# Loading each 128-row block of x in two half-width transfers instead of one

## The chip, the cores and the metric

The kernel runs on one core of one Trainium2 chip. The metric is the device time of one execution in microseconds (us), as a median over runs. A core has five engines with a queue of instructions each: PE (matrix multiplication, whose weight loads are listed as PEld), DVE, ACT, POOL and SP. SP computes nothing here; its queue issues nearly all plain transfers between DRAM and the on-chip memory. POOL issues the indexed transfers (scatter and gather). All transfers are carried out by 16 DMA engines.

## The reference, cut to what matters

`x` is 32 batches of 512 rows (channels) by 1024 columns (nodes), in float32, that is 2.1 MB a batch; `adj` is 512 by 512.

```python
q = einsum('c,bcn->bn', wq, x);  k = einsum('c,bcn->bn', wk, x)
scores = q[:, None, :] + k[:, :, None]
att = softmax(where(scores > 0, scores, 0.01 * scores), axis=-1)
agg = einsum('bcn,bmn->bcm', x, att)
x = layernorm(x + relu(einsum('oc,bcm->bom', adj, agg) + bm[None, :, None]))
x = layernorm(x + einsum('bnf,nm->bmf', x, adj * adj) + bias)
```

## The kernel before, in words

The batches are handled one after the other, with the steps of about four batches interleaved. The softmax over 1024 nodes is not done as a matrix: because a score is the sum of one number per row and one per column, the kernel sorts the nodes by `q`, makes running sums of the sorted rows from both ends, and looks up for each row the place where the score changes sign.

For one batch the steps are as follows. `load` (`ld` in the schedule, line 87) brings x into a tile of 128 partitions by 4 blocks by 1024 columns, one transfer for each block of 128 rows, 512 KB each, issued from SP. `parts` (`pa`, line 247) multiplies x with `wq` and `wk` on PE: block 0 first, then blocks 1, 2 and 3, and within a block four column groups of 256, which PE runs side by side in four quarters of its array. ACT copies the result (`pc`, line 255), SP writes it out and reads it back to all partitions (`qw` and `ro`, lines 275 and 283), and DVE and ACT compute ranks and counts from it (`rk`, line 308, and `ct`, line 323). PE computes `z`, adj times x, transposed (`z`, line 346, and the steps beginning with `z` at line 390, which are a seven-product scheme for half of the columns). POOL scatters the rows of z to their ranks in DRAM (`sc`, line 451). SP reads the sorted rows back (`sl`, line 470), DVE forms the running sums (lines 491 and 501), SP writes them as a table (`tw`, line 553), POOL gathers two entries per node (`g`, line 563), DVE and ACT mix them (`mix`, lines 585 and 590), and PE transposes the mixture (`t`, line 609). DVE adds it to x in place (line 617), ACT normalises x (line 635), and the second layer follows: its sums of quarters on DVE (`T1` to `T4`, lines 646 to 660), its seven-product scheme on PE (lines 667 and 702), its residual, its normalisation, and the store (`st`, line 777).

The order on every engine is written out by hand in three strings of words, `head` (start and batches 0 to 13), `loop` (batches 14 to 18) and `tail`. A word such as `ld.1` calls `load` for the batch one later than the current one. The change doesn't touch these strings, so the words stay in their order.

Three things set when a load can run. The pool `xp` has four tiles, so the load of a batch reuses the tile of the batch four earlier, and its first transfer waits on SP until the last readers of that tile are done, among them `T4` on DVE (line 660) and the last products of the second layer on PE (line 667). The words `ld.1` and `pa.1` stand about 8 us apart in time, so PE asks for the new x soon after. And all plain transfers take turns on eight completion counters: a transfer's issue waits until the transfer eight earlier has landed. Ahead of the loop, where four loads follow one another, these counters hold back the issue.

A part of the loop that shows the load and its neighbours:

```python
    mw.-2.1 t4.-3 ms.-2.4 12.-3.0 ms.-2.6 up.-3.1 ms.-2.7 Y.-3.0 d.-1.4 ld.1 s1.-3.1 mx.-2.6
    zc.0.1 ra.-3.1 Y.-3.1 zc.0.0 lr.-3.0 rb.-3.1 ms.-2.5 up.-3.0 r1.-3.1 sc.0.1 21.-3.0 lr.-3.1
    s1.-3.0 sc.0.0 mx.-2.5 d.-1.3 21.-3.1 ll.-3.0 ra.-3.0 mx.-2.7 n.-3.1 rb.-3.0 d.-1.2 cu.-1
    r1.-3.0 mx.-2.4 ll.-3.1 st.-3.1 d.-1.1 pa.1 uc.-1 ls.-3.1 ls.-3.0 d.-1.0 s1.-3.3 tu.-1.0
```

Of the kernel before, what the change touches and what calls it, by code (L numbers as in the profile page):

```python
# [42 lines left out]
P = 128  # L43
# [6 lines left out]
def adj_resnorm_kernel(  # L50
# [10 lines left out]
    nc = tc.nc  # L61
# [3 lines left out]
    H = 512  # L65
# [18 lines left out]
    def load(b):  # L84
        t = xp.tile([P, CT, N], F32, tag="x", name=f"x_{b}")
        for c in range(CT):
            nc.sync.dma_start(out=t[:, c, :], in_=x[b, c * P : (c + 1) * P, :])
        xts[b] = t


# [16 lines left out]
    for h in range(2):  # L107
        nc.scalar.dma_start(
            out=room[3 - 3 * h : 6 - 3 * h, 0, :],
            in_=bias[h * H : (h + 1) * H].partition_broadcast(3),  # L110
# [665 lines left out]
    def store(b, m):  # L776
# [5 lines left out]
    ops = {  # L782
        "ldw": adj_load, "wt": adj_turn, "wc": adj_copy_odd, "wd": adj_copy_even, "R": adj_sums,
        "ld": load, "pa": parts, "pc": parts_copy, "co": cols, "cc": cols_copy, "ro": row,
        "tb": top, "tp": top_end, "qw": row_out, "rk": rank, "re": rank_end, "ct": count, "ce": count_end,
        "we": weights_exp, "oq": own_q, "z": product, "zc": product_copy, "sc": scatter,
# [497 lines left out]
```

## Time and profile before

| what | value |
|---|---|
| median of 3 runs | 1942.7 us (1941.02 to 1945.48) |
| the profiled execution's own time | 1937.53 us |
| its span | 1935.6 us |
| PE busy | 1887.7 us, 98% of the span |
| DVE / ACT / POOL busy | 1702.7 / 1483.2 / 894.1 us |
| moved by the DMA engines | 558.05 MB, 288 GB/s over the span |
| loads of x | 128 transfers of 512 KB |

The span runs from the first to the last instruction of the profiled execution; 1.9 us of its own time lie around it. An engine that is busy for nearly the whole span can still be held up for short times that matter. The chain of work that ended last tells where: it is followed back from the last instruction to whatever released each step. A queue named q1 carries the plain transfers of SP, q10 those of ACT, and q0 the scatters and gathers of POOL. The records of the DMA engines are packets; a packet of a load of x is one row of one block, 4096 bytes.

### The profile page before, as it was taken

What the parts mean: (1) busy time and instruction counts of PE and PEld (TensorE: products, weight loads), DVE (VectorE), ACT (ScalarE), POOL (GpSimd) and SP (SyncE); (2) the same over time, 40 slices, a digit from 0 to 9 for tenths busy, and PEclk for the clock granted to TensorE, in tenths of its full rate; (3) what the DMA queues carried; (4) which work ended last, traced back from release to release, by engine and by line L of the source; (5) the groups of instructions that cost most, each with busy time, mean ns of one, the idle gap of its engine ahead of it and who ended that gap; (6) DMA issues with size and microseconds to landing.
All of it is one profiled execution on the core that took longest, in us unless ns stands there. A gap on an engine that the chain in (4) does not pass through costs nothing.

```text
span 1935.6 us, 23404 instructions
## 1 busy us (share of the span) xinstructions
PE 1887.7 (98%) x7073; PEld 1072.8 (55%) x7073; DVE 1702.7 (88%) x2746; ACT 1483.2 (77%) x2663; POOL 894.1 (46%) x1074
## 2 busy tenths in 40 slices
PE   7989999999999999999999999999999999999897
PEld 3654556555555555556555556555565555564343
DVE  6898899998899889989988989988999989898983
ACT  3566778888778777778887778877778787877786
POOL 5263535335535345444456444455453455445531
PEclk9999999999999999999999999999999999999999
DMA  6577788777788687877787877777888677887862
GB/s 251 199 296 279 273 330 329 268 293 284 294 332 317 252 309 270 327 297 306 288 305 277 317 305 304 288 297 284 310 310 314 259 294 294 311 316 279 336 244 94
DMA packets 147446, 558.05 MB, mean 288 GB/s; under 512 B 19653, under 2 KB 19793, under 8 KB 139129
## 3 DMA queue, kind: packets, MB, share of 16 engines
q1 hardware_dynamic: 89784, 353.87, 48.3%
q0 software_dynamic: 57344, 202.15, 27.6%
q8 instruction: 56, 0.92, 0.2%
q14 instruction: 70, 0.57, 0.1%
q10 hardware_dynamic: 192, 0.55, 0.1%
HBM read 287.08 MB, written 269.42 MB: 288 GB/s over the span
## 4 chain that ended last, share of the span: by engine, by line
PE 83%; DMA 7%; DVE 5%; ACT 2%; issue 2%; POOL 1%; SPq 0%; DVEq 0%; POOLq 0%; ACTq 0%
PE z_ps L346 20%; PE sum_ps L667 19%; PE pair_ps L667 10%; PE z_sum_ps L390 10%; PE z_pair_ps L390 7%; PE agg_ps L609 5%; PE pair_ps L702 5%; PE qk_ps L247 3%; DMA x<-in_x_dram 2%; DMA table<-tab 2%; DMA tab<-sorted_z 2%; PE carry_ps_False L509 1%; DVE tab L538 1%; PE carry_ps_True L509 1%; DVE junk_v L308 1%
## 5 line engine op out<-in xcount | busy, mean ns | idle before, releaser
L563 POOL DMA_INDIRECT got<-table,of x256 | 302.9, 1183 | 565.5 <-DMA table<-tab 226.2
L346 PE MATMUL z_ps<-adj_t,x 128*128 128x512 f32 x1088 | 486.8, 594 | 1.7 <-ACT adj_t L179 1.0
L451 POOL DMA_INDIRECT sorted_z<-zt,to x256 | 314.9, 1230 | 177.8 <-issue 75.1
L308 DVE SCALAR_TENSOR_TENSOR junk_v<-qb,qkc,tie 128x1024 uint8<-128x1024 f32 x256 | 328.7, 1284 | 12.3 <-DMA x<-in_x_dram 6.7
L346 PEld LDWEIGHTS z_ps<-adj_t,x 128*128 128x128 f32 x1088 | 202.3, 190 | 225.6 <-issue 210.7
L323 ACT ACTIVATE junk_s<-qb,qkc 128x1024 uint8<-128x1024 f32 x256 | 293.4, 1146 | 22.1 <-DMA qb<-q_row 14.1
L667 PE MATMUL sum_ps<-zt,S 128*128 128x512 f32 x512 | 236.1, 593 | 2.3 <-DVE zt L651 1.2
L585 ACT ACTIVATE got<-got,w 128x512 f32<-128x512 f32 x256 | 172.6, 718 | 42.5 <-DVE w L580 42.1
L590 DVE SCALAR_TENSOR_TENSOR got<-got,w 128x512 f32<-128x512 f32 x256 | 185.8, 747 | 11.0 <-ACT got L585 10.6
L491 DVE SCALAR_TENSOR_TENSOR tab<-tab,ac 128x514 f32<-128x514 f32 x192 | 144.7, 753 | 45.4 <-ACT tab L486 29.5
L617 DVE SCALAR_TENSOR_TENSOR x<-agg_ps,small,x 128x1024 f32<-128x1024 f32 x128 | 163.2, 1281 | 23.1 <-PE agg_ps L609 22.8
L600 ACT ACTIVATE junk<-g,tv 128x1024 uint8<-128x1024 f32 x128 | 146.9, 1148 | 34.9 <-DVE g L722 28.6
L501 DVE SCALAR_TENSOR_TENSOR tab<-tab,ac 128x513 f32<-128x513 f32 x224 | 167.8, 749 | 2.3 <-ACT tab L499 1.5
L667 PEld LDWEIGHTS sum_ps<-zt,S 128*128 128x128 f32 x512 | 96.5, 190 | 120.7 <-issue 106.6
L753 POOL TENSOR_SCALAR tv<-tv 128x1 f32<-128x1 f32 x124 | 51.5, 415 | 239.7 <-ACT junk L600 233.6
L774 ACT ACTIVATE g<-g,nb,tv 128x1024 f32<-128x1024 f32 x124 | 151.1, 1237 | 8.2 <-POOL nb L764 8.1
L600 ACT ACTIVATE junk<-x,tv 128x1024 uint8<-128x1024 f32 x128 | 146.9, 1148 | 12.2 <-DVE x L617 9.9
L538 DVE TENSOR_TENSOR tab<-tab,carry 128x2052 f32<-128x2052 f32 x64 | 146.3, 2292 | 4.1 <-ACT carry L516 4.1
L635 ACT ACTIVATE x<-x,tv 128x1024 f32<-128x1024 f32 x128 | 139.3, 1141 | 0.5
L609 PEld LDWEIGHTS agg_ps<-ident,got 128*128 128x128 f32 x1024 | 116.4, 141 | 36.2 <-issue 24.5
L609 PE MATMUL agg_ps<-ident,got 128*128 128x128 f32 x1024 | 129.3, 273 | 2.7 <-DVE g L722 2.0
L667 PE MATMUL sum_ps<-x,adj 128*128 128x512 f32 x256 | 123.4, 605 | 7.2 <-ACT x L635 7.2
(144 smaller groups left out, 3280.9 us busy)
## 6 DMA issues: line engine op xcount, KB each, us to landing
table<-tab SPq DMA_DIRECT2D x64, 2056.0 KB
tab<-sorted_z SPq DMA_DIRECT2D x64, 1028.0 KB
x<-in_x_dram SPq DMA_DIRECT2D x128, 512.0 KB
out_dram<-g SPq DMA_DIRECT2D x128, 512.0 KB
qb<-q_row SPq DMA_DIRECT2D x31, 512.0 KB
sorted_z<-zt,to POOLq DMA_INDIRECT x256, 5.1
got<-table,of POOLq DMA_INDIRECT x256, 7.9
adj_in<-in_adj_dram SPq DMA_DIRECT2D x1, 1024.0 KB
```

Of the source, the lines that this page charges most:

```text
L308: nc.vector.scalar_tensor_tensor(s.junk, s.qb, s.q[:, j : j + 1], tie[:, at : at + N], ALU.subtract, ALU.is_gt, accum_out=s.rank[:, j : j ...
L323: nc.scalar.activation(junk, s.qb, AF.Sign, bias=s.k[:, j : j + 1], accum_out=s.sign[:, j : j + 1])
L346: nc.tensor.matmul(s.z[j], xt[:, c, j * P : (j + 1) * P], adj_t[:, c, :], start=(c == 0), stop=(c == CT - 1),)
L390: nc.tensor.matmul(ps, a[:, i, k * P : (k + 1) * P], v[:, i, :], start=start and i == 0 and (k == 0 or bank == 1), stop=(i == 1), skip_gro ...
L451: nc.gpsimd.indirect_dma_start(out=sorted_z[b % 2][:, :], out_offset=bass.IndirectOffsetOnAxis(ap=s.to[:, j : j + 1], axis=0), in_=zt[:, j ...
L501: nc.vector.scalar_tensor_tensor(v, v, c, s.zs[:, j + 1, 0:D], ALU.mult, ALU.add)
L563: nc.gpsimd.indirect_dma_start(out=s.got[:, j, :], out_offset=None, in_=table[b % 2][:, :], in_offset=bass.IndirectOffsetOnAxis(ap=s.of[:, ...
L585: nc.scalar.activation(down, down, AF.Copy, scale=s.w[:, 1, j : j + 1])
L590: nc.vector.scalar_tensor_tensor(up, up, s.w[:, 0, j : j + 1], down, ALU.mult, ALU.add)
L600: nc.scalar.activation(junk, t, AF.Square, bias=v[0][:, i : i + 1], scale=-float(N), accum_out=v[1][:, i : i + 1],)
L609: nc.tensor.transpose(s.agg[o][:, j * P : (j + 1) * P], s.got[:, j, o * P : (o + 1) * P], ident)
L667: nc.tensor.matmul(ps, a[:, k, g * P : (g + 1) * P], v[:, k, :], start=False, stop=(k == 1), skip_group_check=first is None,)
```

## The change

Each block of 128 rows is loaded by two transfers, one for columns 0 to 511 and one for columns 512 to 1023, in place of one transfer of whole rows. A batch takes eight transfers of 256 KB in place of four of 512 KB. The bytes, the destination and the order of all other instructions stay as they are.

```diff
         for c in range(CT):
-            nc.sync.dma_start(out=t[:, c, :], in_=x[b, c * P : (c + 1) * P, :])
+            for h in range(2):
+                at = slice(h * H, (h + 1) * H)
+                nc.sync.dma_start(out=t[:, c, at], in_=x[b, c * P : (c + 1) * P, at])
         xts[b] = t
```

`H` is 512 and `CT` is 4.

## The prediction

> **What bounds the kernel now.** I read the page first: the busy times, then the chain that ended last.
>
> ```profile
> PE 1887.7 (98%) x7073; PEld 1072.8 (55%) x7073; DVE 1702.7 (88%) x2746; ACT 1483.2 (77%) x2663; POOL 894.1 (46%) x1074
> ...
> PE 83%; DMA 7%; DVE 5%; ACT 2%; issue 2%; POOL 1%; SPq 0%; DVEq 0%; POOLq 0%; ACTq 0%
> ```
>
> PE is nearly always at work and holds 83% of the chain. The table of busy times by stretches shows where its 48 idle us lie: 10 us before 40 us, 9 us between 100 and 180 us, 27 us after 1760 us. In the middle there is nothing left (columns: stretch, its length, then the busy us of PE, PEld, DVE, ACT and POOL with instruction counts, PE's clock, the DMA engines' share, GB/s):
>
> ```profile
> 700.00:1300.00 600.00, 599.66 (x2309) 345.75 (x2308) 542.03 (x870) 478.81 (x856) 295.56 (x339) 1.00 0.79 298
> ```
>
> So a change to the loads counts only where PE would wait for x. The view of line 87 gives what waits today (us, times), and the chain around one such place shows the mechanism (start, length, what):
>
> ```profile
> L87 SPq DMA_DIRECT2D x<-in_x_dram x128: 328/430/1140, 0.8 to 1747.9; - x128
> ...
>   PEld qk_ps L247: 2.1, 4
>   PE qk_ps L247: 0.3, 1
> ```
>
> ```profile
> 925.82 3.45 PE pair_ps L667 x8
> ...
> 929.32 0.35 SPq L87
> ...
> 930.66 7.77 DMA x<-in_x_dram
> 938.44 0.04 issue
> 938.48 0.64 PE qk_ps L247 x8
> 939.12 3.63 PE z_ps L346 x8
> ```
>
> The fourth transfer is issued at 930.66 and lands at 938.44, and PE, in the middle of `parts`, begins its block 3 at that moment. The load is just in time. How nearly so elsewhere can be worked out from the landing events in the trace. In the three loads that PE waits for, the time from PE's first matmul of line 247 to the landing is longer than 1.25 us by just the delay that PE shows, so block 3 is needed 1.25 us after that matmul. Over the 28 loads from batch 4 on, the landing comes 0.68 us before this (median): six have under 0.5 us to spare, nine between 0.5 and 0.8 us, ten more, and three are late, by 0.27, 0.49 and 0.30 us (batches 17, 23, 31). This margin of 0.7 us is what the change spends or spares.
>
> The time line of an ordinary batch shows what shares the DMA engines with the load:
>
> ```profile
> 1104.29 1.77 SPq L87 DMA_DIRECT2D x<-in_x_dram  x4
> 1107.07 1.08 POOL L451 DMA_INDIRECT sorted_z<-zt,to  x1 [0.42 <-ACT got L585]
> 1108.45 1.49 POOL L451 DMA_INDIRECT sorted_z<-zt,to  x1 [0.21 <-issue]
> 1111.25 0.34 SPq L777 DMA_DIRECT2D out_dram<-g  x1
> 1111.89 1.93 PE L247 MATMUL qk_ps<-x,wqk 128*32 128x256 f32 x32
> ```
>
> Two scatters are issued 2.8 and 4.2 us after the load's start. In the DMA records their packets begin about 7.0 us after the load's start; the load's packets end at 7.1 us on the middle DMA engine and at 8.0 us on the last.
>
> **The change part by part.**
>
> *Issue on SP.* Four more issues per load. The first of a row takes 0.35 us, the others 0.43, with 0.04 between (above: four in 1.77 us). Eight take 0.39 + 7 x 0.47 = 3.7 us, 1.9 us more. Behind them on SP stands the store of line 777, issued 7.0 us after the load's start and waiting for ACT, so 3.3 us remain of that cover; without it the store would come 1.9 us later, and nobody waits for it. Does the later issue delay the landing? A first 512 KB transfer lands 3.5 us after its issue and the next ones 1.28 us apart, so some 2.2 us are fixed. The eighth, issued at 3.2 us, would alone land at about 3.2 + 2.2 + 0.65 = 6.1 us; the stream is done at 7.4 us at the earliest. The issue doesn't decide. Cost: nothing.
>
> *Smaller packets.* Rows of 4096 bytes become 2048. Not in the trace for a load of x; nearest are the 2056-byte rows of line 470. The DMA view, first of 12 to 16 us (4 KB rows of x), then of 1139.5 to 1141.5 us (2056-byte rows), then of 19 to 21 us, then of 1142.5 to 1145.5 us (columns: packets, MB, share of the 16 engines):
>
> ```profile
> q1 hardware_dynamic: 454, 1.66, 101.7%
> ...
> q1 hardware_dynamic: 403, 0.80, 104.1%
> ...
> q10 hardware_dynamic: 102, 0.42, 52.1%
> q1 hardware_dynamic: 109, 0.40, 50.3%
> ...
> q0 software_dynamic: 206, 0.78, 65.2%
> q1 hardware_dynamic: 220, 0.45, 39.0%
> ```
>
> The first two give 415 and 400 GB/s. The 2.1 MB of a load take 5.05 and 5.24 us: 0.2 us later. By single records (159 ns for 4096 bytes, 84 for the few 2048-byte rows of adj) it is 32 x 9 ns = 0.3 us. I take 0.25 us.
>
> *Share against the scatters.* The last two windows show the same rule twice. Where both queues carry 4 KB they share evenly; where q1 has 2056 bytes and q0 4112, packets are about equal in number and q0 gets two thirds of the bytes. The end of a load now shares evenly with a scatter; with 2 KB rows it gets a third. A scatter holds an engine for four packets, 0.65 us. On the last engine, which ends at 8.0 us, about 0.5 us of x were left at 7.0 us and let three packets of the scatter between. After, 0.75 us of x are left (9 packets): all four packets of the first scatter go between and perhaps one or two of the second, so it ends at 8.4 to 8.8 us. Bounds for the landing's shift, packets included: 0.2 us (no scatter in the way) and 1.3 us (a whole further scatter, 0.65, in the way, and 0.4 for the rest). I take 0.6 us, nearest to the last engine's count.
>
> *Waits on PE.* Eight waits per `parts` in place of four. The four quarters run side by side, so both halves of a block are needed at once and nothing is won by the finer grain. Matmuls with a wait start at the same 216 ns grid as those without, so I book none; were each extra wait to cost the 7 ns between neighbours, 32 loads would cost 1 us.
>
> *The sum for batches 4 to 31.* The shift minus each load's margin, where positive, summed over the 28: 1 us in all for a shift of 0.3, 3.2 us for 0.6 (12 loads late), 9.8 us for 1.0, 16 us for 1.3. I take +3.2 us.
>
> *The start.* Here the eight counters hold back the issue: the first four transfers are issued at 0.79, 1.25, 1.71 and 4.37 us, the last just after the first landed at 4.35. With halves, less is in flight, yet enough: four halves are 1 MB, 2.5 us of work at 415 GB/s, against 2.2 + 0.65 us from issue to landing. So adj, which PE needs, lands 0.1 to 0.3 us later than its 11.8 us. Against this, the read-back `qb` of the first batch on ACT's queue, issued at 15.3 us, lands at 22.5 behind x; less is ahead of it now and it gets two thirds, so DVE's ranks begin earlier. They release PE at 37.3 us after 0.77 us of idling. That wait can go; late next is PE's own row of matmuls from 16.8 us. Together: -0.7 to +0.3 us, I take -0.4.
>
> *Total.* +3.2 - 0.4 = +2.8 us on the profiled 1937.5: 1940.3 us. The median of the runs stood 5.2 us over the profiled execution, so the median is 1945.5 us, +0.14%.
>
> **A rule weighed.** The gap between landings of the four transfers is 1.28 us, the bare time of eight packets of 159 ns on each engine, so a further transfer in a row costs no fixed time. The Trainium skill, DMA: Bandwidth & Descriptors, section on the anatomy of one DMA, gives about 2.0 us fixed per transfer plus its bytes at 436 GB/s (for transfers issued from GpSimd), and its rules ask for 1 MiB or more per transfer; this speaks against the change. Were the fixed times to add up one after the other, four more would put each landing 8 us later, an estimate from that page of some 200 us in all. The 1.28 us show that they overlap, and I go by the row.
>
> **The rivals.** *Slower: the scatter takes the place of the load's end.* With a shift of 1 us or more, 20 of 28 loads are late, and the sum is 9.8 to 16 us, with the start 1952 to 1958. It decides (over 0.2%) from a shift of about 0.7 us, where the 28 loads cost 4.5 us. For it: two scatters in the last us of nearly every load, and the two-thirds share. Against it: the last engine already lets most of one scatter pass today. Half-rows read from DRAM at a pitch of 4 KB, which no row shows, would add here.
>
> *Faster: the load lands earlier.* In many batches the third landing comes 2.2 us after the second, not 1.28, with no scatter yet at work; if two smaller transfers ran through this without loss, the landing could come earlier. It wins at most the 1.1 us of the three late loads and 0.8 us at the start: 1940.8, still within 0.2%. More would need a cause that I don't see.
>
> *Nothing is split.* The two halves could be one record again; then the time is 1942.7. The DMA records of adj, 2 KB rows inside one transfer, are counted singly, so this is unlikely.
>
> **How the numbers follow.** A measurement of this kernel tells about 0.2% (3.9 us) from no change. My forecast, a shift of 0.3 to 0.7 us, has 0.40, with a range of its own of 1942 to 1946.5; landing earlier within the bound or nothing split 0.08, the scatter rival and what else delays the landing 0.44, a gain of another kind 0.08. So faster 0.08, same 0.48, slower 0.44. The range of 8 in 10 reaches from 1940 (both small gains and some scatter of the runs) to 1958 (a shift of 1.3 us).
>
> **What would show it.** Packets of q1 rise by 16384, with 2048 bytes each. Eight issues per load take about 3.7 us. The waits of PEld and PE in line 247 for x rise from 2.4 us to some 5.6 us in all, and 12 loads or so are waited for. DVE's first rank begins before 22.7 us. I am wrong if these waits stay near 2 us or pass 9 us, if SP's issues exceed 0.6 us each, or if PE's idle time grows outside line 247.

## The result, and the profile after

The changed kernel takes 1967.4 us (median of 4 runs, 1964.72 to 1970.01); the kernel before, on the same chip, 1943.7 us. The ratio is 1.0129 [1.0116, 1.0142]: 24 to 25 us slower. The profiled execution after took 1964.72 us with a span of 1962.8 us, against 1937.53 and 1935.6 us; these 27.2 us of span are what is followed here. Times inside a load are read from the landing events in the traces; a landing is the last event of a transfer. All lines of the code lie two further down (87 is 89, 247 is 249).

The busy times and the chain that ended last, from the page of the changed kernel:

```profile
PE 1903.7 (97%) x7073; PEld 1075.4 (55%) x7073; DVE 1703.6 (87%) x2746; ACT 1485.6 (76%) x2663; POOL 900.8 (46%) x1074
...
PE 67%; DMA 14%; DVE 6%; ACT 5%; issue 4%; SPq 2%; POOL 2%; DVEq 0%; ACTq 0%; POOLq 0%
```

PE does the same 7073 matmuls. Its share of the chain falls by 16 points, and DMA's doubles. The view of the load's line tells who waits (us, times):

```profile
L89 SPq DMA_DIRECT2D x<-in_x_dram x256: 328/431/1566, 0.8 to 1774.4; - x128
...
  PEld qk_ps L249: 27.2, 33
  PE qk_ps L249: 11.4, 17
```

The waits of `parts` for x rise from 2.4 to 38.6 us. (The two rows overlap: a matmul and its weight load can wait for the same landing.) PE in the middle of one batch, from the time line:

```profile
1125.96 1.92 PE L249 MATMUL qk_ps<-x,wqk 128*32 128x256 f32 x28
1128.64 0.62 PE L249 MATMUL qk_ps<-x,wqk 128*32 128x256 f32 x4 [0.76 <-DMA x<-in_x_dram]
```

The last four of the 32 matmul records of `parts` come 0.76 us late, after the last half has landed. The table of busy times by stretches (columns as in the prediction), for the start before, then after, and for the middle after:

```profile
0.00:10.00 10.00, 3.72 (x33) 1.51 (x33) 3.31 (x14) 1.28 (x1) 3.01 (x9) 1.00 0.81 285
10.00:20.00 10.00, 7.36 (x30) 5.14 (x26) 1.56 (x3) 1.45 (x3) 7.74 (x10) 1.00 1.03 414
...
0.00:10.00 10.00, 4.92 (x29) 1.50 (x29) 3.31 (x14) 1.28 (x1) 3.02 (x9) 1.00 0.70 223
10.00:20.00 10.00, 5.26 (x23) 3.99 (x23) 1.56 (x3) 1.45 (x3) 4.72 (x7) 1.00 0.93 323
...
700.00:1300.00 600.00, 593.12 (x2230) 338.95 (x2230) 530.12 (x859) 469.74 (x837) 288.56 (x330) 1.00 0.78 290
```

In the first two stretches of 10 us the DMA engines move 223 and then 323 GB/s, where they moved 285 and 414 before. In the middle, where nothing had been left, PE now idles 6.9 us in 600, and it also does 79 matmuls fewer in that time, since the work has shifted.

Where the time goes is seen from the first matmul of `parts` in some batches (us):

| batch | before | after | later by |
|---|---|---|---|
| 1 | 20.5 | 25.7 | 5.2 |
| 4 | 180.6 | 183.9 | 3.3 |
| 13 | 704.0 | 710.2 | 6.2 |
| 25 | 1403.5 | 1426.8 | 23.3 |
| 31 | 1755.0 | 1779.6 | 24.6 |
| end | 1935.6 | 1962.8 | 27.2 |

There are two parts: some 3 to 5 us at the start, and 17 us from batch 13 to 25, which is 1.4 us a batch. The 32 matmuls of `parts` took 1.93 us before and take 3.33 us in the median batch of 14 to 25. Summed over batches 4 to 31 this growth is 21 us (22.6 over 1.93 us each, after 1.2 before).

The DMA view shows the load's stream. The first line is of 1106.8 to 1110.8 us before, the second of 1120.9 to 1124.9 us after, both 2.5 to 6.5 us after a load's first issue:

```profile
q1 hardware_dynamic: 393, 1.42, 94.8%
```

```profile
q1 hardware_dynamic: 579, 1.04, 88.0%
```

In the same four microseconds 1.04 MB arrive in place of 1.42, that is 260 in place of 355 GB/s. No scatter or gather moves data in either stretch. The median last landing of batches 14 to 25 comes 10.3 us after the first issue; it was 8.3. That is a shift of 2.0 us. PE asks for x as before, 7.6 us after the first issue.

### The profile page after: what moved, and what is told of

The parts are those of the page before. It is cut to its first block, busy times and chain, and to the rows that moved or that the text cites. A ratio compares the mean times of both kernels' runs of the same rounds, so it can differ in the third digit from the quotient of the medians.

```text
span 1962.8 us, 23542 instructions
## 1 busy us (share of the span) xinstructions
PE 1903.7 (97%) x7073; PEld 1075.4 (55%) x7073; DVE 1703.6 (87%) x2746; ACT 1485.6 (76%) x2663; POOL 900.8 (46%) x1074
## 3 DMA queue, kind: packets, MB, share of 16 engines
q0 software_dynamic: 57344, 202.15, 27.2%
## 4 chain that ended last, share of the span: by engine, by line
PE 67%; DMA 14%; DVE 6%; ACT 5%; issue 4%; SPq 2%; POOL 2%; DVEq 0%; ACTq 0%; POOLq 0%
PE z_ps L348 18%; PE sum_ps L669 14%; PE pair_ps L669 8%; PE z_sum_ps L392 8%; DMA x<-in_x_dram 6%; PE z_pair_ps L392 6%; PE agg_ps L611 5%; PE pair_ps L704 4%; DMA table<-tab 3%; DMA tab<-sorted_z 3%; SPq L89 2%; PE qk_ps L249 2%; DVE tab L540 2%; DMA got<-table,of 1%; PE carry_ps_False L511 1%
## 5 line engine op out<-in xcount | busy, mean ns | idle before, releaser
L602 ACT ACTIVATE junk<-x,tv 128x1024 uint8<-128x1024 f32 x128 | 147.1, 1149 | 12.3 <-DVE x L619 9.9
```

The source lines that it names most:

```text
L602: nc.scalar.activation(junk, t, AF.Square, bias=v[0][:, i : i + 1], scale=-float(N), accum_out=v[1][:, i : i + 1],)
```

## The experiments

In all of them "from batch 4 on" means that batches 0 to 3 are loaded in whole rows. The kernel before took 1942.3 us beside the first four, 1944.6 beside the next four and 1942.5 beside the reordered ones. Some expectations give 10.4 to 10.7 us for the landing with halves and 2.4 us for its shift. The reading behind them took a few landing events of later transfers for the load's own; 10.3 and 2.0 us are right. Where a landing time is given below without more, it is the median of batches 14 to 25.

**Start and later loads apart.**

```diff
+            for h in range(2 if b >= 4 else 1):    # from batch 4 on; b < 4 for the other
+                at = slice(h * H, (h + 1) * H) if b >= 4 else slice(0, N)
```

Halves from batch 4 on (waits for x are those of PEld and then of PE, in us):

> The loads of batches 0 to 3 are whole rows again, those of 4 to 31 are halves. In the changed kernel's trace PE begins batch 4 (line 249) 3.3 us later than before, and the rest of its 27 us of span are added after that. If the start and the later loads cost what these marks say, this kernel is 20 to 24 us slower than before (1964 to 1968 us), with the loads' last landing about 10 us after their first issue in batches 14 to 25. If the start's delay had been absorbed later and the later loads cost all of it, it is 24 us or more slower; if the delay from the start were what upsets the later batches, it is under 8 us slower.

Measured: 1963.6 us, 1.0104 [1.0087, 1.0121]; waits for x 23.9 and 11.0 us; last landing 10.3 us. Halves for batches 0 to 3 alone:

> Halves for batches 0 to 3 alone, whole rows from batch 4 on. If the two costs are separate (start about +4 us by the mark of batch 4, +3.3 us in the changed kernel; later loads about +21 us), this run is 3 to 5 us above before, with waits of qk for x back at about 2.4 us. If the late start is absorbed later, it is within 1 us of before. If the slow later loads were an after-effect of the start (the order of loads and stores set there), it would be near +20 us.

Measured: 1946.5 us, 1.0009 [0.9998, 1.002], waits for x 7.2 us, growth of `parts` from batch 4 on none, last landing 8.3 us. So the later loads cost some 20 us by themselves, and the start 2 us (0 to 4). The two add up to 22 of 25 us, within the intervals. The start's 4 us at batch 4 (184.8 us by the mark) are partly given back on the way.

**Transfers, packets or addresses?** Three kernels from batch 4 on: four transfers of half-rows of two blocks (as many transfers as before, with packets of 2048 bytes); eight transfers of columns 0 to 895 and 896 to 1023 (rows cut unevenly); eight transfers of pieces of 2048 bytes that lie side by side in DRAM, for which x arrives permuted.

```diff
+                nc.sync.dma_start(out=t[:, two, at], in_=rows.rearrange("(c p) n -> p c n", p=P))
...
+            for lo, hi in ((0, N - P), (N - P, N)) if b >= 4 else ((0, N),):
...
+                    out=t[:, c, h * H : (h + 1) * H], in_=rows.rearrange("p (k n) -> (p k) n", k=2)
```

> From batch 4 on, four transfers per load of 512 KB as before, but each of half-rows (2 KB) of two blocks: the packets of the change with the number of transfers of before. If the half-rows make the stream slow (theory rows), as slow as halves from batch 4 on: 15 to 24 us slower than before. If the doubled number of transfers does it (theory transfers), within 5 us of before, the rest being the 0.2 to 0.3 us for smaller packets that the prediction had.

> From batch 4 on, eight transfers per load, split at column 896: rows of 3584 and of 512 bytes. Theory transfers: as halves from batch 4 on, 15 to 24 us slower than before, since the number of transfers is that of the change. Theory rows, if a packet costs by its being cut at all: the same. Theory rows, if it is large packets that keep the stream fast: 3 to 12 us slower.

> From batch 4 on, eight transfers of 128 pieces of 2 KB as in the change, but the pieces of one transfer lie next to each other in DRAM (64 whole rows, each cut in two), so x arrives permuted and the output is not the reference's. If what is slow in half-rows is their pitch of 4 KB in DRAM, within 6 us of before. If it is the 2 KB packet or the number of transfers, 15 to 24 us slower, as halves from batch 4 on.

Measured: 1965.5 us (1.0119 [1.0099, 1.014]), 1966.8 us (1.0116 [1.0099, 1.0134]) and 1959.2 us (1.0086 [1.0069, 1.0103]); last landings at 9.7, 10.6 and 9.7 us. Four transfers are as slow as eight, so the number of transfers is not it. Cutting a row unevenly costs as much as halving it. The profiled execution of the adjacent pieces, from which its landing comes, is the one that came down to 1951.3 us; its other three took 1958.7 to 1960.5 us, 16 to 18 us over the kernel before, where halves cost 21. So the pitch in DRAM may carry a part, a fifth or so, but not the whole. What the slow ones share is 64 packets per engine and load in place of 32.

The same count of eight transfers, but of whole rows, 64 each:

> From batch 4 on, eight transfers per batch of 64 whole rows each: as many transfers as the change has, but rows of 4 KB, so 1024 packets of data a batch fewer than with halves. Theory packets (twice as many packets per load slow its stream): within 5 us of before, last landing near 8.3 us after the first issue. Theory transfers (eight issues and eight completions): +15 to +24 us, last landing near 10.5 us. Eight issues take about 3.7 us under both.

```diff
+                nc.sync.dma_start(out=t[up, c, :], in_=rows)    # 64 whole rows
```

Measured: 2038.6 us, 1.0482 [1.0436, 1.0527], last landing 12.3 us. Neither theory foresaw this. The experiment changed something else as well, the partitions that one transfer writes to; the bench below shows how much.

Halves that come from the same four batches of x every time:

> Halves from batch 4 on, but each load reads batch b % 4 again, so that the output is not the reference's. If the middle of the stream is slow because data is read from DRAM for the first time: near before (within 5 us). If it is slow by its packets, wherever they come from: +18 to +24 us, as with halves from batch 4 on (+21).

Measured: 1965.1 us, 1.0109 [1.0091, 1.0126], last landing 10.0 us. The same 8 MB read again and again are no faster.

Larger transfers in place of smaller ones, in all loads:

> All loads: two transfers of 1 MB per batch, whole rows of two blocks each, in place of four: 32 packets of 4 KB per engine as before. Theory packets: the last landing stays near 8.3 us, the first landing of a load moves from about 2.4 us later to the second block's, still ahead of its use except at the first batch; 0 to -3 us by fewer counters held at the start, or up to +3 us where the first batch waits for its first block. If fewer and larger transfers were what counts by themselves: the last landing falls under 8 us and the waits for x go to zero, -1 to -3 us.

Measured: 1944.2 us, 1.0001 [0.9991, 1.0011], last landing 8.2 us, waits for x 8.3 us. Two transfers of 1 MB are worth as much as four of 512 KB: no version here beats the kernel before. The Trainium skill (DMA: Bandwidth & Descriptors, rules for kernel authors) asks for 1 MiB or more per transfer; for transfers queued one behind the other this run shows no gain from it.

**Is it only the wait in `parts`?** Columns 0 to 511 are loaded first, and in 18 of the 28 batches (the expectation says 19) `z` of a column block that lies in them (3.6 us on PE) goes ahead of `parts`. The control does the same with whole rows. What it comes to in the words of the loop:

```diff
-ld.1 ... pa.1 uc.-1 ls.-3.1 ls.-3.0 d.-1.0 s1.-3.3 tu.-1.0 z.1.2
+ld.1 ... uc.-1 ls.-3.1 ls.-3.0 d.-1.0 s1.-3.3 tu.-1.0 z.1.2 pa.1
```

> Halves from batch 4 on, the four left halves (columns 0 to 511) first, then the four right ones; and where z of the same batch follows parts on PE (19 of the 28 batches from 4 on), z of column block 2, which reads left halves alone, goes ahead of parts. z takes 3.6 us, so parts asks for the right halves 3.6 us later than before: the shift of the landing of 2.4 us is covered there. If the slow load costs time only through the wait in parts, most of the +21 us of halves from batch 4 on goes: 0 to +7 us against before (nine batches are not reordered). If the slower load costs otherwise too (later stores, scatters, DVE), +10 us or more stays.

> The same reordering of z ahead of parts with whole rows. z reads the four blocks one after the other and needs block 3 about 1.4 us after its start, nearly as parts does (1.25 us), so nothing is relieved: within 3 us of before. It tells what the reordering does by itself, through parts and its copy coming 3.6 us later: if that delays the ranks, slower by 3 us or more.

Measured: 1970.6 us (1.0145 [1.0128, 1.0162]) and 1965.3 us (1.0115 [1.0099, 1.0132]). The order alone costs 23 us. `parts` and the scores come 3.6 us later, and the chain of 700 to 1300 us in the control then has 9.2% on the DMA of `got<-table,of` (the gather), which was not among its larger parts before; that the delay reaches PE this way is the likely reading, not tested further. Beside its own control, though, halves cost 5 us in place of 21. The waits for x in the kernel with halves, reordered:

```profile
  PEld qk_ps L249: 4.7, 9
  PE qk_ps L249: 0.3, 1
```

The landing was as late as ever (10.6 us); `parts` of batches 14 to 25 took 1.93 us again. So most of the steady cost is the wait in `parts`. Where the other 5 us come from is open, since both kernels of this pair now wait in other places too. As a remedy the reordering failed.

**Does the load lose only while it begins?** One more transfer of 512 KB goes ahead of the load.

```diff
+        if b >= 4:
+            nc.sync.dma_start(out=t[:, CT - 1, :], in_=x[b, 0:P, :])
```

> Halves from batch 4 on, with one more transfer of 512 KB (whole rows, overwritten later) ahead of the eight in the same queue. Theory opening (the stream is slow only while it begins on idle engines, whatever follows): the last landing is 0 to 1 us behind that of the kernel with whole rows and the same transfer ahead. Theory packets (a load of 64 packets per engine is slower by itself): 2.4 us behind it, near 12 us after the first issue. Time in both over +20 us, by the added transfer alone.

> Whole rows, with the same added transfer of 512 KB ahead from batch 4 on: last landing near 9.6 us after the first issue (8.3 + 1.28), of which the third landing gap keeps about 1 us of loss; waits of qk for x make about +16 us, from the sum for a shift of 1.3 us.

Measured, one run each: 2004.6 and 1997.5 us, last landings at 11.9 and 11.3 us. Both were later than expected: the transfers into the block that the added one also writes, the last two of nine and the last of five, are issued only after it has landed, 3.6 to 4.2 us after the first issue, and the end then lies among the scatters. The difference of 0.5 us is what "opening" expected, not the 2.0 us of the unpreceded loads; but with these held issues and the scatters at the end it isn't a clean test.

**The load by itself.** Behind the end of the kernel before, 44 loads, one at a time, with no other DMA traffic:

> The kernel before with 44 more loads of x behind its end, one at a time, each gated by DVE after the load before it, with no other DMA traffic. Cases, four of each: whole rows; halves; four transfers of half-rows of two blocks; halves of adjacent pieces; 64 whole rows each; halves on two queues (SP and ACT); and whole rows and halves with DVE, ACT and PE at work during the load, and halves with one of them at work. Its time is that of before plus some 500 us. Theory packets or opening (the DMA stream loses by itself): quiet halves end 2 us or more later than quiet whole rows (10.4 against 8.0 us after the first issue), and on two queues the loss falls if one queue's descriptors are the limit. Theory engines (the on-chip memory is contended by the engines that work at that time in the loop): quiet halves within 0.5 us of quiet whole rows, halves with the engines at work 2 us later, and the single-engine cases name the engine. If neither shows a loss, it needs other DMA traffic around it.

| case, four each | last landing after the first issue, us |
|---|---|
| whole rows | 7.4 to 7.9 |
| halves | 8.6 to 9.6 |
| four transfers, half-rows of two blocks | 8.6 to 8.9 |
| halves, adjacent pieces | 8.5 to 9.1 |
| halves on two queues, SP and ACT | 8.0 to 8.5 |
| 64 whole rows each | 11.4 to 11.6 |
| whole rows, DVE, ACT and PE at work | 7.6 to 8.5 |
| halves, DVE, ACT and PE at work | 8.9 to 10.0 |
| halves, DVE or ACT or PE at work | 8.7 to 9.6 |

The first table row is four transfers a load, the others as in the experiments above; "at work" means that these engines compute on other data meanwhile. Two loads by the time line (four issues, eight issues), and by the DMA view: first 1.5 to 6.5 us after the first issue of that load of whole rows, then the same stretch of the next, with halves, then six microseconds of a load of 64 rows each:

```profile
2166.22 1.75 SPq L1271 DMA_DIRECT2D bench<-in_x_dram  x4
...
2174.13 3.65 SPq L1287 DMA_DIRECT2D bench<-in_x_dram  x8
```

```profile
q1 hardware_dynamic: 528, 1.97, 98.9%
```

```profile
q1 hardware_dynamic: 837, 1.53, 94.9%
```

```profile
q1 hardware_dynamic: 441, 1.48, 104.3%
```

On idle DMA engines, in an idle core, halves run at 306 GB/s where whole rows run at 394, and land 1.3 us later by the medians (9.0 against 7.7). This is the DMA stream's own loss; half-rows in four transfers have 1.0 us of it. By the medians, engines at work add 0 to 0.45 us, so they are not the cause of the 1.3 us. In the loop the shift is 2.0 us. The remaining 0.7 us lies at the end: the eighth half lands 0.64 us after the seventh in the bench, 1.4 us after it in the loop, where the two scatters begin 7 us after the first issue.

Why more packets lose is not settled. They are not slower as such: in the stream of the first batches, from 12 to 15 us, halves run at some 400 GB/s (from 15 to 20 us, where counters hold back the issue, at 250 to 340). The loads of batches 6 and 10 begin while a gather is moving data; with halves they land at 10.0 and 9.0 us, with whole rows at 10.0 and 9.2. These are two loads, and batch 7, ahead of which only a short piece of a gather runs, does lose (10.8 against 10.0). A load of the bench, which begins on idle engines, loses between 2 and 6 us after its first issue. In those five microseconds each load of halves with no engine at work has 33 to 44 packets of 200 to 940 ns among some 700 that mostly take 84; the whole rows have 13 to 23 of over 200 ns among some 470 that mostly take 159. Two queues lose half as much (8.3 us). There the last issue also begins after 1.6 in place of 3.2 us, but four transfers of half-rows on one queue are issued as early (1.9 us in all) and land at 8.7, so earlier issuing explains 0.3 us at most.

The loads of 64 rows explain the miss above: whole packets of 4096 bytes, the engines fully busy, and 247 GB/s. The Trainium skill (SBUF — State Buffer, door 1: the DMA port swizzle) says that partitions 0 to 63 reach only half of the ports. This run agrees in direction: 0.63 of the rate, with transfers to the two halves of the partitions following one another.

## Why the prediction was wrong, point by point

The direction came true as its second case, "Slower", to which it gave 0.44; but the cause that it named, the scatters, carries 0.7 of the 2.0 us of shift (below); the larger part stood only under "what else delays the landing". The time of 1945.5 us and the range to 1958 us are missed, by 22 and 9 us.

*Right.* The place: PE waits for x in `parts`, and the margin of 0.68 us is what was spent. Eight issues take 3.67 us, as worked out, and don't decide. Extra waits cost nothing by themselves. The count of packets rose by 18432: the 16384 named, and 2048 completion writes:

```profile
q1 hardware_dynamic: 108216, 353.88, 48.3%
```

*Wrong: the step "Smaller packets".* It took 0.25 us, from 2056-byte rows at 400 GB/s. That row and the 4 KB rows beside it were both of streams that had been running for some time, the 4 KB rows behind a queue of loads, the others in the middle of a read-back. The load in question begins on idle engines. There the term is 1.3 us in the bench, five times as much. The trace of before had a sign of it, noted under "Faster" and read the wrong way round: the third landing 2.2 us after the second, with no scatter at work. That was probably the same loss with 32 packets, some 0.8 us in the loop; with 64 it grew.

*Right in kind, half the size: "Share against the scatters".* The rest of the 0.6 us that was taken, 0.35 us, was 0.7 us. The two terms together are 2.0 us in batches 14 to 25, beyond the upper bound of 1.3 us, and so the sum's last entry, 16 us, was passed too: the loads from batch 4 on cost 20 to 21 us. With a shift of 2.0 us in every load the prediction's own margins would give some 32 us. The shift differs from load to load, from -0.2 to 3.1 us with a median of 1.3 over all 28, and it is mostly larger in batches 12 to 25 than elsewhere; one shift for all loads was a simplification of the sum. The bound was not far enough out because its packet term came from rows in full flow.

*Wrong: the step "The start".* It said that with halves less is in flight, "yet enough", and took -0.4 us. The chain of the first 60 us (start, length, what) shows what followed:

```profile
5.83 5.90 DMA x<-in_x_dram
...
11.75 6.56 DMA x<-in_x_dram
...
18.33 0.02 ACTq L285
...
18.39 0.35 ACTq L285
...
18.78 1.08 ACT adj_t L181 x2
...
19.91 5.83 PE z_ps L348 x8
```

The seventh half of the first batch waits for the counter of the third, which lands at 5.44 us; the eighth goes out behind it at 5.83 and lands at 11.73 us. The four whole transfers had landed by 8.67. adj stands behind these issues on SP (first before, then after):

```profile
4.74 0.43 SPq L101 DMA_DIRECT2D adj_in<-in_adj_dram  x1
...
6.31 0.44 SPq L103 DMA_DIRECT2D adj_in<-in_adj_dram  x1
```

It lands at 14.97 in place of 11.80 us, 3.2 us later and not 0.1 to 0.3: about half of that is the later issue, and the rest goes with the slower stream. And `qb`, expected earlier, is itself late: ACT's queue issues it at 18.39 in place of 15.31 us, after a counter that a half of the second batch holds until 18.31 (the row that it reads back lands at 17.56 in place of 15.29, so the counter itself adds 0.8). DVE's first rank begins at 25.25 us, where the prediction asked for less than 22.7. The copies of adj that PE needs stand behind this issue on ACT and begin at 18.78 in place of 15.70 us; that is no more than adj's own delay, since the transposes that they read end at 18.7 in place of 15.5 us.

PE's `z` then begins 3.1 us later, and it also takes 2.1 us longer, which makes the 5.2 us of batch 1 in the table (before, after):

```profile
16.83 3.70 PE L346 MATMUL z_ps<-adj_t,x 128*128 128x512 f32 x8 [0.97 <-ACT adj_t L179]
...
19.91 5.83 PE L348 MATMUL z_ps<-adj_t,x 128*128 128x512 f32 x8 [0.79 <-ACT adj_t L181]
```

The trace of this execution has no record of the granted clock before 24.2 us. The run with halves for the first four batches alone shows the same slow `z` (5.49 us), and there the clock is recorded as half, from 13.6 to 23.8 us (0.50 in the row below; the kernel before has 1.00 in the same stretch):

```profile
15.00:20.00 5.00, 3.79 (x18) 3.38 (x16) 1.56 (x3) 0.92 (x2) 4.76 (x7) 0.50 0.88 314
```

The prediction had no term for this, and what lowers the clock isn't shown by these runs. Halves for the first four batches alone show that 2 us of the late start reach the end.

*What it named as a sign of error* came: waits of 38.6 us, far past 9. As for the rule weighed, the fixed time per transfer does overlap, as the 1.28 us said (with half-rows, four transfers cost as much as eight). The rule's direction held all the same, through the packets.

## What to carry to other kernels

A packet's cost is to be priced from a row with the same beginning: here a stream that started on idle DMA engines was not a stream in flow. Where a load is just in time, more and smaller packets cost at the point of its use what its margin doesn't cover, each batch anew; look for gaps between landings that the bare packet time doesn't explain, since here they grew with the number of packets. Where completion counters are shared, halving transfers halves what can be in flight, and an issue that waits for a counter holds the issues behind it on that queue, as that of adj here (6.31 in place of 4.74 us).

## What was not expected of the hardware

A load of 2.1 MB in rows of 2048 bytes loses 1.3 us against rows of 4096 bytes when it begins on idle DMA engines; two loads that began behind a gather lost nothing against whole rows. Whole rows lose too, up to 0.6 us in the bench and some 0.8 us in the loop. Transfers to 64 partitions run at 247 GB/s with all engines busy, where 128 partitions have 394. And PE at 98% did not mean that its order was free: `parts` put 3.6 us later cost 23 us. At the start, the first eight matmul records of `z` took 5.83 in place of 3.70 us, and a run that shows the same has half of the clock granted there.
